# Loading x and adj a second time in 32-column blocks and transposing them on VectorE, in a four-layer graph network kernel

## The chip, the cores and the metric

The kernel runs on one core of a Trainium2 chip. The metric is the device time of one execution, in microseconds (us). The core has a matrix engine (TensorE, written PE in the profile), VectorE (DVE), ScalarE (ACT), GpSimd (POOL) and SyncE (SP), each of which works through its own instruction stream in order, and 16 DMA engines. Transfers are issued by an instruction on SP or ACT; such an instruction tells the DMA hardware what to move, and the engine goes on. Engines wait for each other and for transfers on semaphores. PE writes its results to PSUM, which DVE and ACT read.

## The reference

There are 32 independent graphs. Each has 512 nodes with 256 features (`x`, 512x256) and a 512x512 adjacency matrix (`adj`, zeros and ones). Four layers follow each other, each with a residual sum and a layer norm:

```python
x = _layernorm(x + _L0_gnn_ref(x, adj, ...))   # masked attention, 8 heads of 32
x = _layernorm(x + _L1_gnn_ref(x, adj, ...))   # relu(((1+eps) x + adj @ x) @ W1 + b1) @ W2 + b2
x = _layernorm(x + _L2_gnn_ref(x, adj, ...))   # h = (eps x + adj @ x) @ W1 + b1; silu(rmsnorm(h)) @ W2 + b2
x = _layernorm(x + _L3_gnn_ref(x, adj, ...))   # softplus(xn @ W_self + (I - s_out*adj*s_in) @ xn @ W_neigh)
```

In layer 0, `q`, `k` and `v` are products of `x` with 256x256 weights, scores are masked where `adj` is 0, and softmax runs over the 512 nodes of a row. Layer 3 uses `s_out` and `s_in`, the inverse square roots of the column sums and the row sums of `adj`. Everything is float32.

A matmul on PE contracts over the partition dimension of both operands. So `q`, `k`, `v` need `x` with features on partitions (`xT`), and every product with `adj` needs `adj` with the summed node on partitions (`adjT`). Both come from memory with rows on partitions.

## The kernel before, in words

Each function call `graph(b)` describes one graph as some hundreds of operations on tiles. 512 nodes are NT = 4 tiles of 128 rows, 256 features are DC = 2 tiles. An operation is recorded with the engines that may run it, an estimated cost in ns, and the tiles it reads and writes.

*What sets the order.* The class `Order` plays all operations of all 32 graphs through a list scheduler on these costs before anything is emitted. An operation's priority is `b * PERIOD` plus a due time; the due time (`due`) lies between the earliest and the latest start of the operation in a single graph, at the share `LATE`. `slot_time` says when a buffer of a pool comes free. The result is one fixed in-order stream for each engine, in which the stages of up to three graphs are interleaved: while PE does the dense layers of one graph, DVE, ACT and SP do the softmax of the next.

*Loads.* `load_x` (L374) and `load_adj` (L377) are issued on SP, 512 KB and 1 MB, into `x_sb` and `adj_sb` (tiles `x`, `adj`), one buffer each. The rows arrive as pieces of 1 KB and 2 KB.

*The transposed copies.* For `adjT` (L556, stage "adjT") PE transposes four 128x128 blocks of `adj` into one PSUM bank `pt_adj`, by a matmul with the identity; ACT copies the bank to `adjT` and sums it along the row in the same instruction, which gives a column of `d_out` (L563). This is done four times in a graph. `adjT` has two buffers, so the copy for graph b can begin when the last product that reads `adjT` of graph b-2, the stage "lap" (`pa_l`, L1299), is done. For `xT` (L585, stage "xT") PE transposes 2x4 blocks of `x` into two banks `pt`, and DVE or ACT copies them (`evacuate`, L512/L513). `xT` has one buffer. The natural `adj` is also read by DVE for the softmax mask `bias` (L573) and the row sums `d_in` (L964).

*Attention.* For 2 head groups of 4 heads and 4 row tiles: PE makes scores `sc` (L680), DVE adds the mask and finds the extreme (`pr`, `mx`, L699), ACT takes the exponential into `pq` (L713), DVE transposes `pq` in 32x32 blocks (L728), SP moves the blocks between partitions with 16 transfers of 64 KB (`pT<-pq`, L739; in graph 0 SP and ACT share them), and PE multiplies with `v` into `po_att` (L777). `pq` and `pT` have two buffers each. So SP issues 128 such transfers for a graph.

*Dense layers.* `ph` (L1037) is the product with `adjT`, `pa` and `pg` (L1054) are first dense layers, `po` (L863) second ones, `pz` (L1258) and `pa_l` (L1299) belong to layer 3. Eight `pg` tiles of layer 2 are copied to `gT` by DVE (L1109) or ACT (L1115). All these results use one PSUM tag of four banks; one of the four is held by `po_att` during a head group, so the next `pg` often has to wait until a bank three results back is copied out. The last activations of layer 3 (L1333, L1336, L1349) are ACT's.

*Semaphores of transfers.* All transfers of the program, on whichever queue, take turns on eight completion counters. An instruction that issues a transfer waits until the transfer before it on the same counter has landed.

Of the kernel before, what the change touches and what calls it, by code (L numbers as in the profile page):

```python
# [11 lines left out]
AF = mybir.ActivationFunctionType  # L12
# [4 lines left out]
P = 128  # L17
# [1 line left out]
LN_EPS = 1e-5  # L19
RMS_EPS = 1e-6  # L20
HEADS = 8
PERIOD = 70000
LEAD = {}


# [27 lines left out]
class Order:  # L53
# [9 lines left out]

    TURN = {"whole": 93, "row": 180, "col": 93}
    TURN_DUE = 0
    LATE = 0.5
    HASTE = 40000

    def __init__(self):
# [30 lines left out]
    def run(self, ops, key, back=False):  # L100
# [32 lines left out]
        done, out = set(), []  # L133

        def slot_time(o):
            t = 0.0
            for x in o.bufs:
                if not x.taken:
                    s = slots.setdefault(x.slot, [0.0] * x.bufs)
                    if not s:  # L140
                        return None
                    t = max(t, min(s))
            return t

        while len(out) < len(ops):
            best = None
            for e, lst in cand.items():
# [3 lines left out]
                for c in lst:  # L151
                    o = c[2]
                    st = slot_time(o)
                    if st is None:
                        continue
                    t = max(free[e], o.ready, st)
                    way = o.ways[c[3]]
                    if e == "DVE" and "port" in way[3] and pool_busy[0] <= t < pool_busy[1]:
                        t = pool_busy[1]
                    k = c[0]  # L160
                    tb = way[3].get("table")
                    if tb and tb != table[0]:
                        k += self.TABLE_DUE
                    if e == "PE" and way[3].get("turn", "whole") != turn[0]:
                        k += self.TURN_DUE
                    if len(o.ways) > 1:
                        f0 = t + way[1]
                        worse = False
                        for j, other in enumerate(o.ways):
                            if j != c[3] and max(free[other[0]], o.ready) + other[1] < f0 - 1:  # L170
                                worse = True
                        if worse:
                            k += 4000
                    opts.append((t, k, c))
# [3 lines left out]
                x = min((x for x in opts if x[0] <= t_min + self.WINDOW), key=lambda x: x[1])  # L178
# [8 lines left out]
            t, e, c = best  # L187
# [22 lines left out]
            for x in o.bufs:  # L210
                if not x.taken:
                    x.taken = True
                    s = slots[x.slot]
# [13 lines left out]
    def due(self, one):  # L227
# [7 lines left out]
        return [  # L235
            (1 - self.LATE) * e + self.LATE * l + LEAD.get(o.stage, 0)
            for e, l, o in zip(early, late, one)
# [27 lines left out]
def kernel(  # L265
# [29 lines left out]
    nc = tc.nc  # L295
    B, N, D = x.shape
    NT = N // P
    DC = D // P
# [13 lines left out]
    ident = const.tile([P, P], F32, name="ident")  # L312
# [11 lines left out]
    for i in range(2):  # L324
        t = const.tile([P, NT, P], BF16, name=f"parts{i}")
# [154 lines left out]
    def graph(b):  # L480
        first, last = b == 0, b == B - 1
        def op(ways, r=(), w=(), hold=()):
            order.op(b, ways, r, w, hold, stage[0])
# [3 lines left out]
        def bank(name):  # L487
            return Buf(ps, [P, 512], F32, "m", f"{name}_{b}", 4)

        def tmp(shape, tag, bufs, name=None, dtype=F32):  # L490
            return Buf(sb, shape, dtype, tag, f"{name or tag}_{b}", bufs)

        def pe(cost, fn, r, w, *hold, turn="whole"):

            op([("PE", cost, fn, {"turn": turn})], r, w, hold)

        def dve(cost, fn, r, w, port=False):
            op([("DVE", cost, fn, {"port": 1} if port else {})], r, w)

        def act(cost, fn, r, w, table=None):  # L500
            op([("ACT", cost, fn, {"table": table} if table else {})], r, w)
# [4 lines left out]
        def either(r, w, dve_way, act_way):  # L506
            op([("DVE", dve_way[0], dve_way[1], {}), ("ACT", act_way[0], act_way[1], {})], r, w)

        def evacuate(dst, src, r, w):
            either(  # L510
                r, w,
                (690, lambda: nc.vector.tensor_copy(dst(), src())),  # L512
                (590, lambda: nc.scalar.copy(dst(), src())),  # L513
            )
# [17 lines left out]
        def small(name, bufs=2, shape=None):  # L532
            return Buf(sb, shape or [P, NT], F32, "s_" + name, f"{name}_{b}", bufs)


        xs = Buf(sb, [P, NT, D], F32, "x_sb", f"x_{b}", 1)
        ad = Buf(sb, [P, NT, N], F32, "adj_sb", f"adj_{b}", 1)
# [8 lines left out]


        stage[0] = "adjT"
        adjT = tmp([P, NT, N], "adjT", 2)
        d_out, d_in = small("d_out"), small("d_in")  # L550
        for m in range(NT):
            pt = bank("pt_adj")

            def tr_adj(m=m, pt=pt):
                for t in range(NT):
                    nc.tensor.transpose(  # L556
                        pt[:, t * P : (t + 1) * P], ad[:, t, m * P : (m + 1) * P], ident
                    )

            pe(460, tr_adj, [(ad,)], [(pt,)], adjT, d_out)  # L560
            act(
                675,
                lambda m=m, pt=pt: nc.scalar.activation(  # L563
                    adjT[:, m, :], pt(), AF.Identity, accum_out=d_out[:, m : m + 1]
                ),
                [(pt,)], [(adjT, m), (d_out, m)],
            )
        allT = [(adjT, m) for m in range(NT)]

# [7 lines left out]
        )  # L577
        stage[0] = "xT"
        xT = tmp([P, DC, N], "xT", 1)
        for c in range(DC):  # L580
            pt = bank("pt")

            def tr_x(c=c, pt=pt):
                for t in range(NT):
                    nc.tensor.transpose(  # L585
                        pt[:, t * P : (t + 1) * P], xs[:, t, c * P : (c + 1) * P], ident
                    )

            pe(460, tr_x, [(xs,)], [(pt,)], xT)
            evacuate(lambda c=c: xT[:, c, :], pt, [(pt,)], [(xT, c)])  # L590
        y = tmp([P, NT, D], "y_att", 2)
        pool(
            2400,
# [7 lines left out]
        v = tmp([P, NT, D], "v", 2)  # L601
# [621 lines left out]
        for c in range(DC):  # L1223
            pt = bank("pt")
            for rt in row_tiles:
# [9 lines left out]
                src = lambda part=part, pt=pt: pt[:, part]  # L1235
                dst = lambda part=part, c=c: xnT[:, c, part]
# [55 lines left out]
        for tp in range(NT // 2):  # L1292
            pa = bank("pa_l")
            for i in range(2):
                t = 2 * tp + i
# [27 lines left out]
        for rt in row_tiles:  # L1323
            part = slice(rt[0], rt[-1] + 1)
            n = len(rt)
# [19 lines left out]
                z0, x3k, port=True,  # L1345
# [22 lines left out]
    for b in range(B):  # L1368
        graph(b)
    with tc.manual_schedule():  # L1370
        order.emit(PERIOD)

# [39 lines left out]
```

## Time and profile before

| | |
|---|---|
| median of three runs | 3604.89 us (3603.01 to 3605.39) |
| the profiled execution | 3604.95 us, of which the traced span is 3603.2 us |
| granted TensorE clock, mean | 0.989 |
| PE busy | 3501.9 us (97% of the span) |
| DVE busy | 2902.0 us (81%) |
| ACT busy | 1836.2 us (51%) |
| POOL busy | 854.7 us (24%) |
| DMA, queue of SP | 253440 packets, 337.79 MB, 36.5% of 16 engines |
| DMA, queue of ACT | 2304 packets, 3.15 MB, 0.4% |

The profile comes from one execution. "Busy" is the time in which an engine ran an instruction; a group's row has the line of the kernel, the engine and operation, the tile written and the tile read, the shapes, the count, the total and the mean of one, and then the idle time of that engine just before these instructions with what ended it. "Chain" means the path followed back from the last instruction to whatever released each step. A DMA row has the number of transfers, the size of each, and the median time from issue to landing. A packet is one contiguous piece that a DMA engine moves; 16 engines share the pieces of a transfer. A granted clock of 1.00 means that PE was not throttled.

### The profile page before, as it was taken

The numbers are of one execution on the slowest core, as the hardware profiler recorded it, in microseconds if no ns is written. First come the engines' busy times: TensorE is split into PE (matmuls) and PEld (weight loads), VectorE is DVE, ScalarE is ACT, GpSimd is POOL, SyncE is SP. The second block draws the span as 40 slices with busy tenths as digits, with TensorE's granted clock in tenths as the row PEclk, the third lists the DMA queues.
The fourth block names the chain that finished last, engine by engine and source line by source line (L and its number), as shares of the span: only waits on it lengthen the run. The fifth ranks groups of instructions, "written<-read, shape, count | busy, mean of one in ns | idle before, by whom it ended". The sixth has DMA issues, their size and how long they took to land.

```text
span 3603.2 us, 60546 instructions
## 1 busy us (share of the span) xinstructions
PE 3501.9 (97%) x20616; PEld 2086.9 (58%) x20616; DVE 2902.0 (81%) x6458; ACT 1836.2 (51%) x3591; POOL 854.7 (24%) x614
## 2 busy tenths in 40 slices
PE   6899999999999999999999999999999999999897
PEld 3455565665565665555655555655656655656464
DVE  6778888888888888887888888888888888887855
ACT  3445554545554545555455555455545455544533
POOL 1112222222222122222122222122222222221221
PEclk8999999999999999999999999999999999999998
DMA  6434333334333333333333333343333343333410
GB/s 174 115 91 109 93 99 100 94 88 106 98 102 97 91 96 101 99 100 93 94 99 98 100 99 95 92 101 100 98 99 95 87 106 99 101 97 79 100 30 12
DMA packets 256052, 344.82 MB, mean 96 GB/s; under 512 B 71552, under 2 KB 107776, under 8 KB 255744
## 3 DMA queue, kind: packets, MB, share of 16 engines
q1 hardware_dynamic: 253440, 337.79, 36.5%
q10 hardware_dynamic: 2304, 3.15, 0.4%
q8 instruction: 165, 2.70, 0.3%
q14 instruction: 143, 1.17, 0.1%
HBM read 55.46 MB, written 16.78 MB: 20 GB/s over the span
## 4 chain that ended last, share of the span: by engine, by line
PE 82%; ACT 5%; SPq 5%; DVE 2%; issue 2%; DMA 1%; ACTq 0%; POOL 0%; DVEq 0%; POOLq 0%
PE po L863 21%; PE ph L1037 11%; PE pg L1054 10%; PE sc L680 6%; PE pa L1054 6%; PE pz L1258 6%; PE pq L614 6%; PE pa_l L1299 6%; SPq L739 5%; PE po_att L777 5%; PE pv L650 3%; ACT L1349 1%; PE pt L585 1%; PE pt L1230 1%; PE pt_adj L556 1%
## 5 line engine op out<-in xcount | busy, mean ns | idle before, releaser
L713 ACT ACTIVATE pq<-pr,mx 128x512 f32<-128x512 f32 x1024 | 729.0, 713 | 437.6 <-DVE mx L699 203.9
L699 DVE CUSTOM_DVE_ANT_0 pr<-sc,bias 128x512 f32<-128x512 f32 x1024 | 665.0, 684 | 205.2 <-PE sc L680 172.7
L728 DVE STREAM_TRANSPOSE pq<-pq 128x2048 f32<-128x2048 f32 x256 | 590.5, 2307 | 41.9 <-ACT pq L713 30.6
L863 PE MATMUL po<-w,gT 128*128 128x256 f32 x2048 | 478.6, 385 | 5.2 <-ACT gT L1193 5.2
L1054 PE MATMUL pg<-hT,w 128*128 128x512 f32 x1024 | 470.8, 599 | 2.2 <-DVE gT L1109 1.1
L863 PEld LDWEIGHTS po<-w,gT 128*128 128x128 f32 x2048 | 387.0, 191 | 111.7 <-issue 54.9
L916 POOL TENSOR_TENSOR rstd<-ve,nhalf 128x4 f32<-128x4 f32 x132 | 132.4, 1003 | 1286.4 <-DVE ve L911 1280.5
L520 POOL TENSOR_TENSOR ssq<-ssq,sq 128x512 f32<-128x512 f32 x219 | 279.4, 1276 | 211.8 <-ACT sq L1130 205.1
L1054 PEld LDWEIGHTS pg<-hT,w 128*128 128x128 f32 x1024 | 187.1, 190 | 235.0 <-issue 212.7
L777 PE MATMUL po_att<-pT,v 128*32 128x128 f32 x8192 | 281.2, 279 | 32.7 <-DMA pT<-pq 22.7
L680 PE MATMUL sc<-kT,qT 32*128 32x512 f32 x2048 | 298.1, 652 | 9.2 <-DVE mx L699 9.2
L777 PEld LDWEIGHTS po_att<-pT,v 128*32 128x32 f32 x8192 | 211.7, 110 | 157.2 <-issue 119.2
L1037 PE MATMUL ph<-adjT,y 128*128 128x512 f32 x512 | 242.9, 599 | 0.1
L1037 PE MATMUL ph<-adjT,y_att 128*128 128x512 f32 x512 | 239.8, 593 | 0.9 <-DVE y L877 0.9
L1054 PE MATMUL pa<-hT,w 128*128 128x512 f32 x512 | 236.3, 605 | 0.0
L863 PE MATMUL po<-w,aT 128*128 128x256 f32 x1024 | 234.6, 382 | 0.0
L1258 PE MATMUL pz<-wsn,xnT 128*128 128x512 f32 x512 | 230.8, 602 | 0.9 <-DVE xnT L1241 0.4
L1299 PE MATMUL pa_l<-zy,adjT 128*128 128x256 f32 x1024 | 227.6, 380 | 1.3 <-DVE zy L1310 1.3
L1299 PEld LDWEIGHTS pa_l<-zy,adjT 128*128 128x128 f32 x1024 | 194.1, 190 | 42.7 <-issue 15.3
L863 PEld LDWEIGHTS po<-w,aT 128*128 128x128 f32 x1024 | 189.7, 190 | 46.2 <-issue 21.9
L563 ACT ACTIVATE adjT<-pt_adj 128x512 f32<-128x512 f32 x128 | 75.2, 590 | 253.9 <-PE pt_adj L556 252.8
L520 POOL TENSOR_TENSOR sp<-sp,y 128x1024 f32<-128x1024 f32 x31 | 73.1, 2358 | 551.6 <-ACT sp L1349 551.5
(141 smaller groups left out, 5251.1 us busy)
## 6 DMA issues: line engine op xcount, KB each, us to landing
pT<-pq SPq DMA_DIRECT2D x4048, 64.0 KB, 2.0
adj<-in_adj_dram SPq DMA_DIRECT2D x32, 1024.0 KB, 5.8
x<-in_x_dram SPq DMA_DIRECT2D x32, 512.0 KB, 4.0
out_dram<-sp SPq DMA_DIRECT2D x31, 512.0 KB, 3.0
pT<-pq ACTq DMA_DIRECT2D x48, 64.0 KB, 2.2
w<-in_L_gnn_W_dram SPq DMA_DIRECT2D x2, 1024.0 KB, 8.2
w<-in_L_gnn_W_dram SPq DMA_DIRECT2D x2, 512.0 KB, 5.9
out_dram<-sp SPq DMA_DIRECT2D x2, 256.0 KB, 2.1
```

The source lines that it names most:

```text
L520: lambda: nc.gpsimd.tensor_tensor(dst(), dst(), src(), ALU.add), {},
L614: nc.tensor.matmul(pq(), lhsT=w[:, c, m * P : (m + 1) * P], rhs=xT[:, c, :], start=(c == 0), stop=(c == DC - 1),)
L680: nc.tensor.matmul(sc[:, j, :], lhsT=qT[hp, g, t * P : (t + 1) * P], rhs=kT[hp, g, :], start=True, stop=True,)
L699: lambda t=t, j=j, sc=sc, pr=pr: nc.vector.tensor_tensor_reduce(out=pr(), in0=sc[:, j, :], in1=bias[:, t, :], scale=-1.0, scalar=3.0e38, o ...
L713: lambda t=t, j=j, pr=pr, pq=pq: nc.scalar.activation(pq[:, :, j].rearrange("p a c s -> p c a s"), pr().rearrange("p (c a s) -> p c a s", ...
L728: lambda pq=pq: nc.vector.transpose(pq().rearrange("p a j c s -> p (a j c s)"), pq().rearrange("p a j c s -> p (a j c s)"),),
L777: nc.tensor.matmul(po[j * HD : (j + 1) * HD, t * P : (t + 1) * P], lhsT=v[:, c, h * HD : (h + 1) * HD], rhs=pT[:, :, j, c, :], start=(c == 0),
L863: nc.tensor.matmul(po[:, i * D : (i + 1) * D], lhsT=lhs[:, k, t * P : (t + 1) * P], rhs=w[:, k, :], start=(i == 0 and k == 0), stop=(i == ...
L1037: nc.tensor.matmul(ph(), lhsT=xin[:, m, c * P : (c + 1) * P], rhs=adjT[:, m, :], start=(m == 0), stop=(m == NT - 1),)
L1054: nc.tensor.matmul(pa(), lhsT=w[:, c, m * P : (m + 1) * P], rhs=hT[:, c, :], start=(c == 0), stop=(c == DC - 1),)
L1258: nc.tensor.matmul(pz(), lhsT=xnT[:, c, t * P : (t + 1) * P], rhs=wsn[:, c, :], start=(c == 0), stop=(c == DC - 1),)
L1299: nc.tensor.matmul(pa[:, i * D : (i + 1) * D], lhsT=adjT[:, m, t * P : (t + 1) * P], rhs=zy[:, m, D : 2 * D], start=(m == 0), stop=(m == N ...
```

## The change

The transposes on PE go, and with them their PSUM banks. `adj` and `x` of each graph are read from memory a second time, straight into `adjT` and `xT`. `load_blocks` issues one transfer for each quarter q of the partitions (32 partitions), from ACT's queue: four for `adjT` (256 KB each) and four for `xT` (128 KB each). The source is cut into runs of 32 float32 columns, 128 bytes, and these are laid out so that a 32x32 transpose in place completes the 128x128 transposes. DVE does that: two instructions on 128x1024 elements for `adjT`, one for `xT`. ACT's pass over `adjT` stays, now in place from SBUF to SBUF, since it yields `d_out`. The natural loads on SP stay, as `bias`, `d_in` and the residual read them. Two constants of the scheduler change with it (`PERIOD`, `LATE`), and `slot_time` now counts how many buffers of one tag an operation takes.

```diff
--- before.py
+++ after.py
@@ -19,7 +19,7 @@
 LN_EPS = 1e-5
 RMS_EPS = 1e-6
 HEADS = 8
-PERIOD = 70000
+PERIOD = 68000
 LEAD = {}
 
 
@@ -63,7 +63,7 @@
 
     TURN = {"whole": 93, "row": 180, "col": 93}
     TURN_DUE = 0
-    LATE = 0.5
+    LATE = 1.0
     HASTE = 40000
 
     def __init__(self):
@@ -133,13 +133,14 @@
         done, out = set(), []
 
         def slot_time(o):
-            t = 0.0
+            t, of = 0.0, {}
             for x in o.bufs:
                 if not x.taken:
                     s = slots.setdefault(x.slot, [0.0] * x.bufs)
-                    if not s:
+                    n = of[x.slot] = of.get(x.slot, 0) + 1
+                    if len(s) < n:
                         return None
-                    t = max(t, min(s))
+                    t = max(t, min(s) if n == 1 else sorted(s)[n - 1])
             return t
 
         while len(out) < len(ops):
@@ -546,24 +547,35 @@
 
 
         stage[0] = "adjT"
+        def load_blocks(dst, src, q):
+
+            v = src.rearrange("(i r) (m a c) -> a r m i c", r=32, a=4, c=32)
+            nc.scalar.dma_start(dst[32 * q : 32 * q + 32].rearrange("r m (i c) -> r m i c", c=32), v[q])
+
         adjT = tmp([P, NT, N], "adjT", 2)
         d_out, d_in = small("d_out"), small("d_in")
+        for q in range(4):
+            op(
+                [("ACT", 600, lambda q=q: load_blocks(adjT(), adj[b], q), {"lat": 6000})],
+                [], [(adjT, m, q) for m in range(NT)],
+            )
+        for m0 in range(0, NT, 2):
+            dve(
+                1200,
+                lambda m0=m0: nc.vector.transpose(
+                    adjT[:, m0 : m0 + 2].rearrange("p m i -> p (m i)"),
+                    adjT[:, m0 : m0 + 2].rearrange("p m i -> p (m i)"),
+                ),
+                [], [(adjT, m, q) for m in range(m0, m0 + 2) for q in range(4)]
+                + [(adjT, m) for m in range(m0, m0 + 2)], port=True,
+            )
         for m in range(NT):
-            pt = bank("pt_adj")
-
-            def tr_adj(m=m, pt=pt):
-                for t in range(NT):
-                    nc.tensor.transpose(
-                        pt[:, t * P : (t + 1) * P], ad[:, t, m * P : (m + 1) * P], ident
-                    )
-
-            pe(460, tr_adj, [(ad,)], [(pt,)], adjT, d_out)
             act(
                 675,
-                lambda m=m, pt=pt: nc.scalar.activation(
-                    adjT[:, m, :], pt(), AF.Identity, accum_out=d_out[:, m : m + 1]
-                ),
-                [(pt,)], [(adjT, m), (d_out, m)],
+                lambda m=m: nc.scalar.activation(
+                    adjT[:, m, :], adjT[:, m, :], AF.Identity, accum_out=d_out[:, m : m + 1]
+                ),
+                [], [(adjT, m), (d_out, m)],
             )
         allT = [(adjT, m) for m in range(NT)]
 
@@ -577,17 +589,19 @@
         )
         stage[0] = "xT"
         xT = tmp([P, DC, N], "xT", 1)
-        for c in range(DC):
-            pt = bank("pt")
-
-            def tr_x(c=c, pt=pt):
-                for t in range(NT):
-                    nc.tensor.transpose(
-                        pt[:, t * P : (t + 1) * P], xs[:, t, c * P : (c + 1) * P], ident
-                    )
-
-            pe(460, tr_x, [(xs,)], [(pt,)], xT)
-            evacuate(lambda c=c: xT[:, c, :], pt, [(pt,)], [(xT, c)])
+        for q in range(4):
+            op(
+                [("ACT", 600, lambda q=q: load_blocks(xT(), x[b], q), {"lat": 4000})],
+                [], [(xT, c, q) for c in range(DC)],
+            )
+        dve(
+            1200,
+            lambda: nc.vector.transpose(
+                xT().rearrange("p c i -> p (c i)"), xT().rearrange("p c i -> p (c i)")
+            ),
+            [], [(xT, c, q) for c in range(DC) for q in range(4)]
+            + [(xT, c) for c in range(DC)], port=True,
+        )
         y = tmp([P, NT, D], "y_att", 2)
         pool(
             2400,
```

## The prediction

> **What bounds the kernel now.** I read the page's busy times first, then the shares of the chain that ended last, then PE's waits between 200 and 3300 us, where the graphs repeat.
>
> ```profile
> PE 3501.9 (97%) x20616; PEld 2086.9 (58%) x20616; DVE 2902.0 (81%) x6458; ACT 1836.2 (51%) x3591; POOL 854.7 (24%) x614
> PE 82%; ACT 5%; SPq 5%; DVE 2%; issue 2%; DMA 1%; ACTq 0%; POOL 0%; DVEq 0%; POOLq 0%
> PE pt L585 <- ACT gT L1115: 13.5, 26, 0.5
> ```
>
> PE sets the time. Of 3100 us it waits only about 16, and the one wait that counts stands just before the transposes of `x`: 13.5 us in 26 graphs, 0.5 each. So PE work that goes shortens the run, and any new wait of PE lengthens it. A reordering can gain almost nothing here, as there is no idle time to fill.
>
> The chain prices what PE loses. `pt` began at 1799.42 in one graph and at 1908.37 in the next, so a graph takes about 109 us.
>
> ```profile
> 1888.49 6.91 PE pa_l L1299 x32
> ...
> 1897.12 0.44 PE pt_adj L556 x4
> ...
> 1908.37 1.09 PE pt L585 x8
> 1909.47 1.72 PE pg L1054 x4
> ```
>
> **What is removed.** Per graph four groups `pt_adj` at 0.44 us (1.75), two banks `pt` (1.09 together) and the wait ahead of them (13.5/32 = 0.42): 3.26 us of PE. Times 30 graphs (the first and last are not full periods): **-98 us**. The copies of `xT` on DVE and ACT go too.
>
> **What is added on DVE and ACT.** DVE gets three transposes of 128x1024. The nearest row is its own transpose at twice the size, so I take half, 1.16 us each.
>
> ```profile
> L728 DVE STREAM_TRANSPOSE pq<-pq 128x2048 f32<-128x2048 f32 x256 | 590.5, 2307 | 41.9 <-ACT pq L713 30.6
> L563 ACT ACTIVATE adjT<-pt_adj 128x512 f32<-128x512 f32 x128 | 75.2, 590 | 253.9 <-PE pt_adj L556 252.8
> ```
>
> That is 3.5 us against 1.3 for the copies that go. The changed order also shifts copies between DVE and ACT; counted with these rows DVE stands at about 95 us of a period of 106. It does not become the bound by its work. ACT's pass over `adjT` stays at 0.59 each (bounds 0.5 and 0.75 for SBUF in place of PSUM); ACT is half idle, so 0.
>
> **What is added in transfers.** Eight transfers per graph on ACT's queue, in pieces of 128 bytes: 512x16 = 8192 for `adj`, 512x8 = 4096 for `x`. The natural loads of the same bytes come in 2 KB and 1 KB pieces:
>
> ```profile
> pT<-pq SPq DMA_DIRECT2D x4048, 64.0 KB, 2.0
> adj<-in_adj_dram SPq DMA_DIRECT2D x32, 1024.0 KB, 5.8
> x<-in_x_dram SPq DMA_DIRECT2D x32, 512.0 KB, 4.0
> ```
>
> No row has 128-byte pieces. At the start of the program biases are loaded in 4-byte pieces. Two windows count packets there, 46.80 to 47.60 and 13.80 to 15.80 us; SP's timeline shows the issues:
>
> ```profile
> DMA packets 289, 0.03 MB, mean 32 GB/s; under 512 B 272, under 2 KB 288, under 8 KB 288
> ```
> ```profile
> DMA packets 671, 0.38 MB, mean 192 GB/s; under 512 B 322, under 2 KB 663, under 8 KB 671
> ```
> ```profile
> 13.33 0.47 SPq L362 DMA_DIRECT2D b_c<-in_L_gnn_b_dram  x1
> 13.84 2.77 SPq L348 DMA_DIRECT2D b_r<-in_L_gnn_b_dram  x1
> ```
>
> In the first, 289 pieces take 0.8 us, 2.8 ns each over all engines together, while the engines were only a third busy (32.7%): something ahead of the engines hands pieces out one by one. The second gives 3.0. And the issue that follows a load of 1024 pieces is held 2.77 us, again 2.7 ns a piece. I take **3.0 ns per piece**, because three rows agree; the ends 2.4 and 3.4 are a margin of mine around them. Against it: pieces already handed out drain faster, 637 in the 0.4 us from 19.40 (0.63 ns each). And if only the engines' own time counted, the three rows above fit 1.75 us plus 13 ns a piece and 56 ns per KB on each of 16 engines, about 20 ns for 128 bytes, so 8192/16 x 20 ns = 10 us. That is the middle case.
>
> "DMA: Bandwidth & Descriptors" of the Trainium skill, section "Why small descriptors are slow (HBM only)", charges each packet 3 cycles beside its 32-byte beats, so a 128-byte one moves at 4 cycles in 7. By that rule 1 MB would take about 4.7 us, an estimate from the 394 GB/s that the window from 1904.8 to 1906.4 us shows, and the kernel would come to about 3530 us; the rows of 4-byte pieces speak against it, and no run here has shown the 128-byte size.
>
> **When the pieces are wanted.** The changed order is the same for graphs 3 to 29 (27 graphs). Let t=0 be the end of the last `pa_l` of graph b-2, which frees the `adjT` buffer that the block loads of graph b wait for. PE then has seven groups of four products (three halves of `ph`, two `pq`, two `pg`) at 1.72 us: 12.04 us. The third `pg` needs the bank of the first. Four banks turn, and `po_att` holds one. The first `pg` is copied to `gT` by DVE, and in DVE's order this copy stands *behind* the first `adjT` transpose, which waits for all four block loads. So PE resumes at t_L + 1.16 (transpose) + 0.74 (`gT` copy) + 0.25 (handing over), where t_L is the landing of the blocks.
>
> t_L: ACT issues the first block at 1.3, after exponentials; 1.0 to first data (in this trace an adj load issued at 1902.33 brought data at 1903.3); 8192 x 3.0 ns = 24.5; 0.8 from the last piece to the waiting engine (estimate: a 64 KB move's 2.0 less 1.0 and its few pieces). t_L = 27.6, PE resumes at 29.75, stall 29.75 - 12.04 = **17.7 us per graph, times 27 = +478 us**. Behind the waiting transpose on DVE lie `gT`, the next scores' `pr` and the statistics; they are late by the same time, not by more.
>
> ACT's own queue: if each issue is held until the block before it has been handed out, the fourth goes out at about 20 us and the copy `hT` between the third and fourth at about 14. The first `pg` waits for that copy, but ends long before 27.6, so 0. SP issues moves of `pT` meanwhile; some wait for a block's landing by the shared completion counters. `po_att` has 17 us before it needs them: 0, and up to 12 us a graph if the cover is gone. The transposes of `xT` may hold DVE 2 to 7 us later in the graph, but the `y` sums behind them are not due until 20 us on: 0.
>
> Start: before its first copy (12.1 us before) ACT now issues `xT` and two sets of `adjT` blocks, each waiting for one before it, and the first moves queue behind those: 24.5 + 12.3 us of pieces, partly beside the weight loads. I take +40 (bounds 5 and 60). End: 0.
>
> Sum: 3604.95 + 478 - 98 + 40 = **4025 us**. The profiled run is within 0.1 us of the median, so this stands for the median.
>
> **The ends.** At 3.4 ns a piece and with SP's 512 pieces of moves and the next adj load taking turns between them, t_L is 32.7 and the stall 22.8: 3605 + 616 - 98 + 60 = 4183. At 2.4 ns t_L is 22.8, the stall 12.9: 3895.
>
> **Rivals.** (1) *The middle case*: engine time binds, 10 us for the blocks, with the natural adj load (5.8 us) sharing the engines. t_L is about 17, the stall 7, 27 x 7 = 190, start +20: about 3720 (3620 to 3800). For it speaks the fast drain; against it the engines' idleness in the first window. (2) *The blocks land in time*, the other side: only the 98 us and a little of the start remain. It needs t_L below about 10, under 0.9 ns a piece. From 1.15 ns (t_L 12.5, stall 2.6, 27 x 2.6 = 70, start +25) it breaks even with what is saved. Then 3605 - 98 + 20 = about 3530. Only the drain row speaks for it. (3) *SP's moves behind the pieces*: if moves of 32 pieces queue behind whole blocks of ACT, `pT` is late by up to 12 us a graph on top: 4025 + 27 x 12 = about 4350. Against it: the two queues have separate rows in the page. (4) *DVE the bound*: 95 us of 106, not reached.
>
> **How the numbers follow.** Chances: the hold-up of 3 ns a piece 0.68, (1) 0.14, (2) 0.13 faster and 0.03 near no change, (3) 0.02. The range reaches from the low end of (1), 3620, to the upper end of the forecast, 4190; the forecast's own range is 3890 to 4190. A measurement tells about 0.2% (7 us) from no change. Faster 0.13, same 0.03, slower 0.84.
>
> **What would show it.** Right: PE's waits have a line `pg` <- DVE `gT` of some 17 us per graph; DVE's first `adjT` transpose waits for DMA; the four blocks land some 8, 14, 20 and 26 us after the first issue; `pt_adj` and `pt` of `x` are gone; ACT's queue has some 390000 packets; PE's share falls to about 85%; the new transpose takes 1.16 us. Wrong: blocks that land within 10 us, PE waits that stay at 0.5 us, a period of 106 us; or a stall that stands at `po_att` <- DMA `pT` instead.

## The result and the profile after

The changed kernel took 3797.35 us (median of four runs, 3791.34 to 3809.07), the kernel before 3604.01 us beside it: a ratio of 1.0543 (95% interval 1.053 to 1.0555). It is slower, as forecast, but by 193 us and not by 420. The profiled execution took 3791.34 us, its span is 3789.6. The page's busy times:

```profile
PE 3460.5 (91%) x19848; PEld 2013.2 (53%) x19848; DVE 2867.4 (76%) x6394; ACT 1888.9 (50%) x3687; POOL 856.6 (23%) x614
```

PE executes 768 instructions less, the 24 transposes of 32 graphs, and its share falls from 97% to 91%. PE's waits from 200 to 3500 us (us in total, times, longest):

```profile
PE po L877 <- ACT qT L649: 37.2, 27, 2.0
PE pg L1068 <- DVE gT L1123: 34.6, 24, 3.2
PE pq L628 <- ACT hT L514: 32.5, 27, 2.8
PE ph L1051 <- DVE zy L1324: 30.3, 27, 1.1
PE sc L694 <- DVE mx L713: 20.1, 27, 2.3
PE pv L664 <- DVE oT L513: 15.1, 27, 0.6
PE pa_l L1313 <- DVE zy L1324: 13.2, 28, 0.7
```

Before there was one such row that counted, 13.5 us. Now there are seven of 13 us and more (the rows left out have 8.5 us and less), nearly all with 27 times: once in each of the 27 graphs whose order is the same. The forecast wait, `pg` on DVE's `gT`, is there, but it is 1.4 us a graph and one among many.

To see where the time lies, take the start of the first `pz` of graphs 0 to 30 in PE's timeline, 30 periods between the first and the last (the last graph is hurried and follows closer). Before, the first is at 245.5 us and the last at 3531.3; after, 274.7 and 3722.7. So the start loses 29 us, the 30 periods lose 162 (the mean of the 5th to the 28th goes from 109.2 to 114.4, the median of all from 108.9 to 114.0), and what follows gains 5.

These 30 periods before and after (start and end, length, busy us of PE, PEld, DVE, ACT and POOL, granted clock, DMA share, GB/s):

```profile
245.49:3531.30 3285.81, 3253.17 (x19140) 1940.33 (x19137) 2685.74 (x5982) 1707.95 (x3326) 807.14 (x572) 1.00 0.37 95
274.75:3722.70 3447.95, 3218.05 (x18445) 1874.04 (x18441) 2637.93 (x5905) 1765.38 (x3429) 807.85 (x572) 0.99 0.43 103
```

PE's idle time, the length less its busy time, rises from 32.6 to 229.9 us. Its busy time falls by 35 us only, where the transposes that went were 30 x 2.84 = 85.

The stretch that the prediction worked out, in the timeline of PE of one graph (start, length, then the idle time before and its cause):

```profile
1666.62 3.72 PE L1313 MATMUL pa_l<-zy,adjT 128*128 128x256 f32 x16 [0.45 <-DVE zy L1324]
1670.17 1.88 PE L1051 MATMUL ph<-adjT,y 128*128 128x512 f32 x4
1673.17 1.98 PE L1051 MATMUL ph<-adjT,y 128*128 128x512 f32 x4 [1.12 <-DVE zy L1324]
1676.20 1.98 PE L628 MATMUL pq<-xT,wq 128*128 128x512 f32 x4 [1.04 <-ACT hT L514]
1678.02 1.88 PE L1051 MATMUL ph<-adjT,y 128*128 128x512 f32 x4
1679.73 1.88 PE L628 MATMUL pq<-xT,wk 128*128 128x512 f32 x4
1681.45 3.60 PE L1068 MATMUL pg<-hT,w 128*128 128x512 f32 x8
1686.10 3.70 PE L1068 MATMUL pg<-hT,w 128*128 128x512 f32 x8 [1.06 <-DVE gT L1123]
```

and of ACT, its queue and DVE in the same graph:

```profile
1671.56 0.59 ACTq L553 DMA_DIRECT2D adjT<-in_adj_dram  x1
1672.19 3.32 ACTq L553 DMA_DIRECT2D adjT<-in_adj_dram  x2
1675.56 0.58 ACT L514 COPY hT<-ph 128x512 f32<-128x512 f32 x1 [3.24 <-issue]
1675.58 1.56 ACTq L553 DMA_DIRECT2D adjT<-in_adj_dram  x1
1684.17 1.25 DVE L565 STREAM_TRANSPOSE adjT<-adjT 128x1024 f32<-128x1024 f32 x1 [1.77 <-DMA adjT<-in_adj_dram]
1685.34 0.71 DVE L1123 TENSOR_SCALAR gT<-pg,b_c 128x512 f32<-128x512 f32 x1
```

`pa_l` ends at 1670.34 (t=0). The first block is issued at t=1.2 (forecast 1.3). The four blocks land 3.7, 5.8, 7.8 and 12.4 us after the first issue (forecast 8, 14, 20 and 26), and DVE starts on them at 1684.17, t_L = 13.8 (forecast 27.6). PE resumes at t=15.8; the forecast's rule, t_L + 2.15, gives 15.95 with the measured t_L. Seven groups of products at 1.72 us fill 12.04, so this stretch loses 15.8 - 12.04 = 3.7 us and not 17.7. (In the 24 graphs in which `pg` waits for `gT`, PE resumes at t = 15.4 to 18.4.) Two pieces of the 3.7 us lie earlier than forecast: `ph` waits 1.1 us for `zy`, and `pq` 1.0 for `hT`, since ACT's queue is held for 3.32 us by the second and third block and `hT` stands behind them. The wait for `gT` still ends last, so these two do not come on top.

What the blocks cost the DMA engines, in windows from 1673 to 1679 us and from 1680 to 1682 (packets in all, then by queue; q10 is ACT's, q1 SP's):

```profile
DMA packets 7098, 1.32 MB, mean 220 GB/s; under 512 B 6874, under 2 KB 6874, under 8 KB 7098
q10 hardware_dynamic: 6762, 0.86, 91.3%
```
```profile
DMA packets 702, 0.76 MB, mean 380 GB/s; under 512 B 353, under 2 KB 353, under 8 KB 702
q1 hardware_dynamic: 349, 0.71, 93.2%
```

In the first window a piece takes 6.0 us / 6762 = 0.89 ns over all engines; the pieces' own times add up to 91.3% of the time of the 16 engines. In the second the natural `adj` load of a later graph is on SP's queue, and in this window the queues take turns packet for packet: 353 of 128 bytes against 349 of 2 KB. For those 2 us a piece takes 5.7 ns. This fits the fourth block, which lands 4.6 us after the third, where the others are 2.0 to 2.1 apart.

### The profile page after: what moved, and what is told of

The parts are those of the page before. It is cut to its first block, busy times and chain, and to the rows that moved or that the text cites. A ratio compares the mean times of both kernels' runs of the same rounds, so it can differ in the third digit from the quotient of the medians.

```text
span 3789.6 us, 59299 instructions
## 1 busy us (share of the span) xinstructions
PE 3460.5 (91%) x19848; PEld 2013.2 (53%) x19848; DVE 2867.4 (76%) x6394; ACT 1888.9 (50%) x3687; POOL 856.6 (23%) x614
## 5 line engine op out<-in xcount | busy, mean ns | idle before, releaser
L877 PE MATMUL po<-w,gT 128*128 128x256 f32 x2048 | 487.7, 387 | 55.6 <-ACT qT L649 37.2
L1313 PE MATMUL pa_l<-zy,adjT 128*128 128x256 f32 x1024 | 238.6, 385 | 14.3 <-DVE zy L1324 13.2
L514 ACT COPY hT<-ph 128x512 f32<-128x512 f32 x60 | 35.1, 586 | 367.9 <-PE ph L1051 275.8
```

The costliest lines, as they stand in the source:

```text
L877: nc.tensor.matmul(po[:, i * D : (i + 1) * D], lhsT=lhs[:, k, t * P : (t + 1) * P], rhs=w[:, k, :], start=(i == 0 and k == 0), stop=(i == ...
L1313: nc.tensor.matmul(pa[:, i * D : (i + 1) * D], lhsT=adjT[:, m, t * P : (t + 1) * P], rhs=zy[:, m, D : 2 * D], start=(m == 0), stop=(m == N ...
```

## The experiments

Two theories. *Pieces*: the loss is the block loads, which hold ACT's queue and DVE. *Order* (the plan): the scheduler's order for the changed set of operations makes PE wait at many places, and the loads are the smaller part.

### The price of a piece

`m1_loads_alone` computes no graph. Loads follow each other with a wait between (the code shortened):

```python
for q in range(4):                      # four quarters of one adj, 8192 pieces of 128 B, on ACT, then on SP
    eng.dma_start(full[32*q : 32*q+32].rearrange("r m (i c) -> r m i c", c=32), v[q])
# 2048 pieces of 4 B to 128 partitions, to 32; 2048 of 128 B to 128; 2048 of 64 B; 1024 of 256 B
# the natural 1 MB load on SP, which ran beside quarters on ACT; last, two quarters on ACT beside two on SP
```

> No graph is computed; loads of different piece sizes follow each other, each alone. If pieces are handed out at one price whatever they hold, as the prediction took it (3.0 ns), 2048 pieces of 4, 64 and 128 bytes all take about 6 us from first to last, and four quarters of adj 24 us. If the price is that of the 128-byte pieces in the changed kernel's trace (about 0.8 ns, 8192 pieces in some 6 to 7 us where no other load shares the engines), 2048 take 1.7 us and four quarters 7 us; the 4-byte ones then show whether they are dearer (2.8 ns) by their size or by going to 128 partitions.

Its DMA windows 23 to 28 us (four quarters of 128-byte pieces on SP), then 30.4 to 31.2 and 31.2 to 32.2 (start and middle of 2048 pieces of 4 bytes):

```profile
DMA packets 6776, 0.86 MB, mean 172 GB/s; under 512 B 6776, under 2 KB 6776, under 8 KB 6776
```
```profile
DMA packets 193, 0.00 MB, mean 1 GB/s; under 512 B 193, under 2 KB 193, under 8 KB 193
```
```profile
DMA packets 1832, 0.01 MB, mean 7 GB/s; under 512 B 1832, under 2 KB 1832, under 8 KB 1832
```

A 128-byte piece takes 5.0 us / 6776 = 0.74 ns, a 4-byte one 0.55 ns in the middle of its load. But the first 0.8 us of the same load hold only 193 pieces, 4.1 ns each. That is what the prediction took for a price: its window from 46.80 to 47.60 us held one load of 256 pieces and nothing of a steady flow, and its window from 13.80 to 15.80 counted pieces that shared the engines with a weight load. From issue to the waiting instruction four quarters alone take 8.2 us on SP (21.17 to 29.41).

These prices are means over stretches with gaps. The steadiest stretches, two quarters on each queue (57 to 60 us) and the 4-byte pieces to 32 partitions (34.5 to 35.1), give 0.60 and 0.38 ns; the third line is the natural load beside quarters on ACT (14.5 to 16.5):

```profile
DMA packets 5022, 0.64 MB, mean 213 GB/s; under 512 B 5022, under 2 KB 5022, under 8 KB 5022
DMA packets 1582, 0.01 MB, mean 11 GB/s; under 512 B 1582, under 2 KB 1582, under 8 KB 1582
DMA packets 366, 0.75 MB, mean 375 GB/s; under 512 B 0, under 2 KB 0, under 8 KB 366
```

Two quarters on each queue take 8.0 us from issue to the waiting instruction, four on ACT's alone 8.3: a second queue hardly helps, so the price lies in what the queues share and not in one queue's hand-out. One load of 2048 pieces takes 2.8 to 3.2 us, whether they have 4, 64 or 128 bytes and go to 32 or 128 partitions, so neither made the 4-byte pieces dear. And turns packet for packet are no rule: in the third line only the natural load moves, though blocks were under way on ACT beside it (one was held 4.8 us at its issue there).

`e3_long_pieces` keeps each instruction of the changed kernel where it was and reads contiguous rows:

```diff
-v = src.rearrange("(i r) (m a c) -> a r m i c", r=32, a=4, c=32)
-nc.scalar.dma_start(dst[32*q : 32*q+32].rearrange("r m (i c) -> r m i c", c=32), v[q])
+v = src.rearrange("(q r k) d -> q r (k d)", q=4, r=32)
+nc.scalar.dma_start(dst[32*q : 32*q+32].rearrange("r m n -> r (m n)"), v[q])
```

> The changed kernel, with the same transfers in the same places and of the same size, but read as contiguous rows, so that a 256 KB transfer has long pieces in place of 2048 of 128 bytes; adjT and xT then hold other values, and the output is not the reference's. Every instruction of PE, DVE and ACT is where it was. 'Pieces': 3797 falls to 3560 to 3620 us. 'Order': only the waits behind hT (1.2 us a graph) and behind the first adjT transpose (1.4 us a graph) go, about 70 us, so 3710 to 3740 us.

3704.05 us (ratio to before 1.0276, 1.0246 to 1.0306): *order* was nearer. The issues of the blocks (min, median, max in ns), in the changed kernel and then with long pieces:

```profile
L553 ACTq DMA_DIRECT2D adjT<-in_adj_dram x128: 590/1525/4212, 7.1 to 3640.7; - x128
```
```profile
L553 ACTq DMA_DIRECT2D adjT<-in_adj_dram x128: 317/342/2143, 4.1 to 3548.9; - x128
```

An issue on ACT is held 1.5 us at the median, which is 2048 x 0.74 ns. The first block of a graph is held 0.59 us only (timeline above), and a lone load of 2048 small pieces in m1 0.33 to 0.37 us. So it looks as if the queue takes a block only as the one before it flows out. PE's waits with long pieces:

```profile
PE po L877 <- ACT qT L649: 35.3, 26, 2.3
PE ph L1051 <- DVE zy L1324: 30.3, 27, 1.1
PE sc L694 <- DVE mx L713: 21.4, 32, 2.4
PE pv L664 <- DVE oT L513: 15.1, 27, 0.6
PE po_att L791 <- DMA pT<-pq: 14.7, 6, 7.4
PE pa_l L1313 <- DVE zy L1324: 12.6, 28, 0.6
```

The rows `pg` on `gT` and `pq` on `hT` (67.1 us together) are gone, so these two were the pieces. The run is 93 us shorter, 3.3 us in the period (111.1). The other five stand nearly as they were. They have nothing to do with the length of a piece. A wait of `po_att` for `pT` is new, 14.7 us in six places. The first `pz` is at 270.2 us and the last at 3632.3, and between them:

```profile
270.20:3632.30 3362.10, 3202.46 (x18445) 1877.42 (x18441) 2620.30 (x5905) 1765.98 (x3429) 807.19 (x572) 0.99 0.42 106
```

### The plan

`e1_constants_alone` and `e10_period_alone` put the constants into the kernel before; `e2_old_constants` takes them out of the changed one.

```diff
-PERIOD = 70000        # e1, e10; the reverse in e2
+PERIOD = 68000
-LATE = 0.5            # e1 alone; the reverse in e2
+LATE = 1.0
```

> The kernel before with only PERIOD = 68000 and LATE = 1.0; the transposes stay on PE. Theory 'pieces' (the loss comes from the 128-byte block loads, which hold ACT's queue and DVE's adjT transposes): the order costs little, 3600 to 3625 us. Theory 'order' (most of the loss comes from the order in which the scheduler now puts the copies, so that PE waits 0.3 to 1.4 us at six or seven places in each graph): the same small waits appear here, 3680 to 3760 us.

> The kernel before with PERIOD = 68000 alone. The two constants together cost it 280 us. If LATE does that (due times moved to the latest start, so that the softmax chain begins too late for po_att), this run stays within 15 us of 3604. If PERIOD does it (graphs packed closer than PE can work them off), 3800 to 3890.

> The changed kernel with the old constants, PERIOD = 70000 and LATE = 0.5; the block loads stay. 'Pieces': the waits behind the loads stay, 3730 to 3800 us. 'Order': most of the loss goes, 3560 to 3680 us.

The constants cost the kernel before more than the whole change: 3885.12 us with both (1.0778, 1.0725 to 1.0832), 3870.40 with PERIOD alone. PERIOD alone does nearly all of it. The changed kernel with the old constants takes 3707.57 us (1.0286, 1.0256 to 1.0316). PE's largest waits with PERIOD alone in the kernel before, and its 30 periods:

```profile
PE pm_t L823 <- DVE parts L805: 60.7, 25, 2.7
PE po L863 <- ACT xT L513: 60.5, 15, 4.8
PE ph L1037 <- DVE zy L1310: 39.4, 27, 1.8
```
```profile
249.10:3800.30 3551.20, 3336.18 (x19131) 1991.93 (x19125) 2762.64 (x6013) 1706.71 (x3291) 797.58 (x572) 0.98 0.34 88
```

Again waits that come back, 15 to 27 times, of 1.5 to 4 us at the mean, with all of PE's transposes in place. They are not its whole loss: in its 30 periods PE idles 215.0 us in place of 32.6, and the same work keeps PE busy 83 us longer, at a granted clock of 0.98 in place of 1.00.

`e6_long_old`: long pieces and old constants.

> Old constants and both block loads, but read as contiguous rows with long pieces (adjT and xT hold other values); the order of instructions is that of the run with the old constants, 3707 us. If the pieces cost here what they cost with the new constants (93 us), 3600 to 3625 us. If with the old constants the order alone is left, 3670 to 3705 us.

3679.03 us. Here the pieces are worth 29 us only: what they cost depends on the plan that they stand in. With the old constants PE's largest wait is `po_att` for the transfers of `pT`, 50.3 us with the short pieces and 57.2 with the long ones, so it is not the pieces that hold these up.

Spacing was then widened: `f1_after_73` and `f2_after_78` (the changed kernel, LATE = 0.5), and `f4_before_73` as a control.

> The changed kernel with LATE = 0.5 and PERIOD = 73000 (3707 us at 70000, 3797 as it was changed). If the added work itself makes the waits, 3690 to 3720 us whatever the plan. If the plan makes them, the time moves by more than 30 us, to either side: 3560 to 3670 where the plan suits, up to 3900 where not.

> As the run before, with PERIOD = 78000. Added work: 3690 to 3720 us again. Plan: another value, 3560 to 3900 us.

> The kernel before with PERIOD = 73000 alone (3604 us at 70000, 3870 at 68000). If graphs packed closer than their work takes are what costs, a wider spacing costs nothing, 3595 to 3615 us. If any other plan is worse, 3650 us or more.

3708.78, 3687.20 and 3750.58 us. For the changed kernel this spoke for the added work, within 22 us of each other. The control spoke for the plan: the kernel before loses 147 us at a wider spacing too, so 3604 is one good plan among bad ones. `f6_after_72_04` settled it: the changed kernel with PERIOD = 72000 and LATE = 0.4.

> The changed kernel, all its operations, with PERIOD = 72000 and LATE = 0.4. If the plan decides, the period falls below 109 us and only the start (some 25 to 35 us) is lost: 3570 to 3640 us. If the added work binds, 3685 to 3710 us as in the three plans with LATE = 0.5.

3622.00 us (1.0052, 1.0035 to 1.0069). All operations of the change are in it, and of 193 us only 19 are left. The first `pz` is at 276.4 us, 31 later than before; the 30 periods take 3273.7 us, 12 less. The periods, then PE's waits:

```profile
276.40:3550.10 3273.70, 3206.18 (x18441) 1865.38 (x18437) 2731.13 (x5907) 1756.02 (x3428) 796.83 (x571) 1.00 0.46 109
```
```profile
PE pr_r L850 <- ACT mT L845: 23.2, 54, 1.2
PE po_att L791 <- DMA pT<-pq: 19.8, 7, 8.1
PE po L877 <- DVE oT L862: 11.5, 28, 0.4
PE pm L1154 <- POOL ssq L521: 9.6, 27, 2.8
```

No row of block loads or of copies behind them is left among them. Five plans of the same operations gave 3622 to 3797 us.

### What PE's relief is worth

`e8_less_pe`: the kernel before, its order untouched, with less work for PE.

```diff
 for k in range(k0, k0 + step):
+    if nk == 8 and k % 4 == 2:
+        continue
     nc.tensor.matmul(po[:, i * D : (i + 1) * D], ...
```

> The kernel before, its order of instructions untouched, but layer 2's second product (po over gT) leaves out 2 of its 8 chunks, so that its output is not the reference's: eight products of 0.43 us, 3.46 us of PE per graph, about what the change takes away (3.26). If PE alone sets the period and the rest has room, 3605 - 31 x 3.46 = about 3498 us. If the rest of the graph's work (exponentials, DVE's transposes, SP's moves, each with two buffers) sets a period close to 109 us whatever PE does, 3560 to 3600 us; then no removal of PE's transposes can bring its 98 us.

3521.08 us (0.9776, 0.9757 to 0.9796), 81 us less where 107 were expected. So PE does set the period, and most of its relief is paid out; the rest turns into small waits, the largest of them 15.6 us of `po` on ACT's `gT`. By the same share some 74 of the change's 98 us would be paid out in a plan as good as the one before (98 x 81/107, an estimate).

### One load at a time, and the start

`e4_adj_alone` and `e5_x_alone` have the old constants and one of the two block loads.

> Old constants; only adjT comes by block loads, xT by PE's transposes as before. It takes 1.75 us of PE per graph away. If the adj blocks are what is left of the loss at the old constants (3707 us: pieces that share the engines with the pT moves, ACT held at the issue), 3670 to 3710 us. If any new plan of the stages costs as much, whichever loads are in it, 3640 to 3700 for this and for x alone alike. If only the start costs, 3590 to 3620.

> Old constants; only xT comes by block loads, adjT by PE's transposes as before. It takes 1.09 us of PE and a wait of 0.42 us per graph away, some 45 us in all. If the adj blocks carry the loss, 3560 to 3600 us, faster than before. If any new plan costs as much, 3640 to 3700 us.

3620.23 us (1.0053, 1.0033 to 1.0072) and 3649.95 us (1.013, 1.0101 to 1.0159). The larger load costs less than the smaller: in these two plans neither the bytes nor the pieces rank them. With adj alone the 5th to 28th periods are 108.7 us at the mean, below the 109.2 before, and the first `pz` is 21 us late.

`e7_start_on_pe` gave graphs 0 and 1 to PE, and let block loads wait for the natural `adj` from graph 2 on.

> Old constants and both block loads, but graphs 0 and 1 have their copies from PE's transposes, so that no block load stands ahead of the first work on ACT; from graph 2 on the scheduler lets a block load go only once the natural adj of that graph is there. If the start costs some 40 us, as the prediction had it and as the count of matmuls in the first 200 us says, 3655 to 3675 us in place of 3707. If the loss is in the period, 3690 to 3715 us.

3853.70 us. The start was repaired (first `pz` at 242.1), but the plan after it has a wait of 145.5 us of `pm` on POOL's `ssq`, 28 times; so this run tells of the plan and says nothing on the price of the loads. `e9_adj_from_2` did the same for adj alone (graph 31 also kept PE's transposes), with the scheduler's wait on `adjT` of the graph before; `e11_costs` told the scheduler the measured costs of a block load, `f3_adj_73` and `f5_adj_71_03` are e9 in two other plans.

> adjT by block loads (old constants, xT by PE), but graphs 0, 1 and 31 keep PE's transposes of adj, and a block load waits in the scheduler until adjT of the graph before is there. The run with adj alone (3620 us) had a period of 108.7 us against 109.2 before and lost 21 us ahead of its first pz. If the start is what it loses, 3590 to 3605 us. If the plan moves again, anything from 3600 to 3700.

> As the run before but one (adjT by block loads from graph 2 on), with the scheduler told what the trace showed for a block load: 1500 ns on ACT in place of 600 and 9000 ns to landing in place of 6000. If the waits behind the loads come from these two estimates, 3570 to 3600 us. If the order of the other stages decides, no better than the run with the old estimates, within 20 us of it.

> adjT by block loads in graphs 2 to 30, xT by PE (3598 us at PERIOD 70000), with PERIOD = 73000. If the plan decides, a suiting one brings the most that 1.75 us of PE in 29 graphs can, 3604 - 51 = 3553 us, a bad one 3650 or more. If the loads themselves bind, 3590 to 3605 us.

> adjT by block loads in graphs 2 to 30, xT by PE, with PERIOD = 71000 and LATE = 0.3. If the plan is what decides, one that suits takes the period to about 107.5 us (109.2 less 1.75): 3555 to 3590 us. If the added work binds, 3598 us as at the best plan so far, or more.

e9: 3597.63 us, ratio 0.9991 (0.9981 to 1.0001), no measurable difference from before; its first `pz` is at 250.2, these periods are 108.4. The others: 3658.65, 3723.98 and 3642.49 us. Better numbers for the scheduler made it worse by 61 us, so they do not by themselves bring a better plan. No version beat the kernel before by more than its interval.

## Why the prediction was wrong in size

**PE as the bound** held: e8 pays out three quarters of such a relief. **The 98 us** held as an upper bound only: in the three runs with both loads whose periods are shown, PE's busy time falls by 35 to 51 us and not by 85.

**The price of a piece failed.** "I take 3.0 ns per piece, because three rows agree": alone it is 0.74 ns (0.60 where it flows steadily), in the kernel 0.89, and 5.7 while the natural load takes turns. Nothing ahead of the engines hands pieces out at 3 ns. The first row was a ramp, the second a window shared with a weight load; the third, the held issue, stood behind that same load in SP's queue, which I did not test by itself. The row that I set aside, 637 pieces in 0.4 us (0.63 ns), was the right one, and the middle rival (engine time) the mechanism that the runs support: 0.74 x 16 = 12 ns of an engine for each piece, where it said 20. With 0.74 ns alone t_L would have been 1.3 + 1.0 + 6.1 + 0.8 = 9.2 and the stall nothing, as in rival (2); what brought it back is the natural load beside the fourth block, which the middle rival had and the forecast left to its upper end.

"DMA: Bandwidth & Descriptors" of the Trainium skill, "Why small descriptors are slow (HBM only)", which the prediction weighed, charges 3 cycles a packet beside its beats and was nearer than my rows: 4.7 us for 1 MB as an estimate, against 6.1 measured (8192 x 0.74 ns) or 4.9 at the steadiest (8192 x 0.60). By its cycles a 4-byte packet would stand to a 128-byte one as 4 to 7, or 0.57, an estimate. Measured are 0.38 / 0.60 = 0.63 in the steadiest stretches and 0.55 / 0.74 = 0.74 in the longer ones.

**When the pieces are wanted** held: the place, the copy `gT` behind the waiting transpose, the first issue, and the sum. With t_L 13.8 in place of 27.6 the same line gives 3.9 us, the trace 3.7. From this one graph the term is then about 27 x 3.7 = 100 us in place of 478. The 1.1 us that `ph` waits for `zy` in this stretch stays with long pieces; e3 is 93 us faster in all.

**ACT's queue at 0** held in the graph shown: `hT` was held and `pq` waited for it, 32.5 us in all graphs, but the wait for `gT` that follows ends last, and it ends with the blocks and not with `hT`. Only in the 3 of 27 graphs without a wait for `gT` does it stand by itself. **SP's moves at 0** held in the changed kernel, where `po_att` waits for `pT` 0.4 us in all, though not in other plans (e2: 50.3).

**The order at nothing failed**, the second error, of the other sign. I read "a reordering can gain almost nothing" from PE's idle time, and did not price what it can lose. With long pieces the 30 periods take 3362.1 us (3632.3 - 270.2) against 3285.8 before, 76 more, though 98 us of PE's work and waits are gone by the chain's rows: 174 us, 5.8 a graph, have come in. PE's idle time shows 140 of them (159.6 - 32.6, and 13 for the wait that went), in waits like `po` on `qT` and `ph` on `zy`. The other 34 are busy time: it fell by 51 us where 85 were taken out. A wait also stretches the products beside it (in the timeline above four take 1.98 us between two waits and 1.72 in a row without), and the granted clock is 0.99 against 1.00; the runs do not separate the two. Together, -98 + 174 + 86 for the pieces (3448.0 - 3362.1) make the 162 of the changed kernel. f6 removes most of the waits with every operation kept, and e10 makes such waits in the kernel before. That the plan makes them is thus shown; which of the scheduler's choices makes a plan good stays open.

**The start** held: +29 us against +40 (bounds 5 and 60). **DVE as no bound** held: 76% busy; a transpose takes 1.24 us, estimated 1.16. ACT's pass takes 0.62, estimated 0.59.

## What to carry to other kernels

A rate is read in the middle of a long transfer that has the queue and the engines to itself; a window that holds one short load shows its ramp. Where a planner with priorities writes the order, a change is a change of plan too: run the plan's constants alone on the kernel before, and the new operations in a few plans, before an operation is blamed. An engine that is 97% busy can gain little from reordering and lose much.

## What the runs showed of the hardware

A piece of 4 bytes costs more than half of what one of 128 bytes costs: 0.38 and 0.60 ns over 16 engines where they flow steadily, 0.55 and 0.74 over longer stretches (m1). A lone load of 2048 small pieces holds the issuing engine 0.33 to 0.37 us, the first of a row of blocks 0.59 to 0.69 (m1); behind another such load on the same queue it is 1.5 us at the median, and 0.34 us where the same bytes have long pieces (the changed kernel and e3). Beside a load of 2 KB packets small pieces slow down: in one stretch of the changed kernel the two queues took turns by packets, and a piece went from 0.89 to 5.7 ns, more than sixfold; in one of m1 none moved for 2 us. What decides between the two was not tested.
